# Two-layer graph network: heads, output and norm of the attention layer for two tiles at once, in stages

## The chip, the cores and the metric

The kernel runs on one core of one Trainium2 chip. The metric is the device time in microseconds (us), the median over runs. Below, DVE is VectorE, ACT is ScalarE, POOL is GpSimd, PE is TensorE, and SP is SyncE, whose queue issues plain loads.

## The reference, cut to what matters

There are 4096 nodes of 128 features and a symmetric 0/1 adjacency of 4096 x 4096 with some 64 neighbours in a row. Layer 0 is graph attention with 8 heads, layer 1 takes quantiles over each node's kept neighbours.

```python
Wh = jnp.einsum('nd,hde->hne', nodes, W)
f1 = jnp.einsum('hnd,hd->hn', Wh, a1); f2 = jnp.einsum('hnd,hd->hn', Wh, a2)
e = jax.nn.leaky_relu(f1[:, :, None] + f2[:, None, :], negative_slope=ALPHA)
att = jax.nn.softmax(jnp.where(mask, e, -9e15), axis=-1)
h = jax.nn.elu(jnp.einsum('hnm,hmd->hnd', att, Wh))
cat = jnp.transpose(h, (1, 0, 2)).reshape(N, NHEADS * DIM)
x = jax.nn.elu(cat @ W1 + b1)
out = _layernorm(nodes + x, gamma, beta)      # layer 0; layer 1 follows
```

Layer 1 gathers each node's neighbours in `out`, sorts them feature by feature, takes three quantiles, and applies one matrix and a residual.

## The kernel before, in words

Layer 0 is `gat`, layer 1 is `sparse`; a flag that is read between them chooses `sparse` (or a dense path that isn't run here), so no instruction of `sparse` starts before `gat` has ended. The change touches `gat` and the class `Front` alone.

*The front* (`Front`) turns adjacency into neighbour lists. `scan(t)` (L352) loads a tile of 128 rows in four quarters on SP's queue, makes 0/1 of them on ACT (a Relu at L361 that looks for negative entries, and a sign at L368), and packs 16 columns into one word with 16 products on PE into one PSUM buffer (L370). `first` (L379) draws the largest words of a tile on DVE in 13 rounds of a maximum and a replacement (`drain8`, L175). `second` peels the bits of four (or three) tiles, a last drain makes lists, and `place(b)` (L427) ranks the nodes of a block of 4 or 6 tiles by their neighbour count and scatters their lists by rank into `rows_d` (L519, POOL). `pieces` (L682) makes a list of these steps; `advance(2)` issues two of them after each half tile of the attention, `through(0)` all of block 0 ahead of it.

*The attention* goes over 32 tiles of 128 ranked nodes, each in two halves, u = 0 to 63. A half has four groups of 16 nodes; a group has 8 partitions a node and r neighbour rows in each (r = 7 to 13, by the block's bounds). `load(u)` (L845) gathers one row for each partition with an indirect DMA on POOL's queue (L858), 28 to 45 of them a half, 2250 in all, into buffers that hold two groups (`nb`, five buffers of up to 24 rows). The indices come from `rows_d` through SP's queue (`indices`, L816: `ids` at L823, `info` at L828). `own_row` (L835) gathers a tile's own rows. `probabilities` (L905) is the softmax: logits on DVE (L935), leaky ReLU with ACT (L943), maxima, an exponential on ACT (L955), sums over a node's 8 partitions. `rows_sum` (L963) spreads the probabilities into matrices of up to 7 rows a time on DVE (L974, two buffers) and multiplies them with the gathered rows on PE (L981) into `ps_z`, which ACT copies to `zT` (L994). After the second half `combine` (L1000) applies the heads' matrices (L1007), ELU (`elu`: a minimum on DVE, an exponential on ACT at L1245, a sum and maximum on DVE), the output matrix (L1010), the second ELU, the norm, and scatters the tile's result into `x1_d` (L1037, POOL).

*What sets the order.* Each engine takes its instructions in one order that is fixed at compile time from the program's order and from when inputs and buffers are expected to be free; independent steps of the front fill in. POOL's and SP's queues are in order as well. `issue_after` holds a half's softmax on DVE and ACT behind the sums of the half before, or behind the whole of `combine`. `load(u + 3)` is issued ahead of half u. An `nb` buffer is free again when PE has multiplied its rows.

The main loop:

```python
for u in range(2 * NT):
    t, half = divmod(u, 2)
    if u + 3 < 2 * NT:
        held[u + 3] = load(u + 3)
        if half and t + 2 < NT:
            mes[t + 2] = own_row(t + 2)
    with ExitStack() as order:
        for ins in behind:
            order.enter_context(tc.issue_after(ins))
        if not half:
            f1 = spread_f1(t, mes[t])
            zT = tp.tile([P, H, P], F32, name="zT", bufs=1)
        e = probabilities(u, held[u], f1)
    behind = rows_sum(u, held.pop(u), e, zT)
    if half:
        behind = combine(t, mes.pop(t), zT)
    advance(2)
```

Of the kernel before, what the change touches and what calls it, by code (L numbers as in the profile page):

```python
# [38 lines left out]
F32 = mybir.dt.float32  # L39
F16 = mybir.dt.float16  # L40
BF = mybir.dt.bfloat16
# [54 lines left out]
SPREAD = 7  # L96
# [206 lines left out]
class Front:  # L303
# [3 lines left out]
    def __init__(self, tc, nc, c, adj, meta_d, ctx):  # L307
# [3 lines left out]
        self.psum_w, self.psum_c = pool("fr_ps", 2, space=PSUM), pool("fr_ps1", 1, space=PSUM)  # L311
# [40 lines left out]
    def scan(self, t):  # L352

        nc = self.nc
        ps_w = self.psum_w.tile([P, NG1], F32, name="ps_words")
        quarter = N // 4
        for i in range(4):
            a_i = self.tp.tile([P, quarter], I32, name="a_i", bufs=3)
            nc.sync.dma_start(out=a_i, in_=self.adj[ts(t, P), ts(i, quarter)])
            nz = self.tp.tile([P, quarter], BF, name="nz", bufs=3)  # L360
            nc.scalar.activation(  # L361
                nz,
                a_i,
                AF.Relu,
                scale=-1.0,
                accum_out=self.negative[:, 4 * t + i : 4 * t + i + 1],
            )
            nc.scalar.sign(nz, a_i)  # L368
            for b in range(4):
                nc.tensor.matmul(  # L370
                    ps_w,
                    self.pows[:, 4 * i + b, :],
                    nz[:, ts(b, NG1)],
                    start=i + b == 0,
                    stop=i + b == 6,
                )
        self.words[t] = ps_w
# [49 lines left out]
    def place(self, b):  # L427
# [47 lines left out]
        for lhs, to in ((self.every, sums[0]), (self.before, inside)):  # L475
            ps = self.psum_c.tile([P, max(BLOCKS) * NC], F32, name="ps_c")
# [191 lines left out]
    def verdict(self, flag_d):  # L668
# [5 lines left out]
        ps = self.psum_c.tile([P, max(BLOCKS) * NC], F32, name="ps_c")  # L674
# [7 lines left out]
    def pieces(self, order_d, flag_d):  # L682

        out = []
        scans = iter(range(NT))
        ahead = lambda: [self.scan(t) for t in [next(scans, None)] if t is not None]
        out.append((None, ahead))
        for b, n in enumerate(BLOCKS):
# [7 lines left out]
            while at < START[b] + n:  # L696
# [9 lines left out]
                for j in range(m):  # L706

                    def one_(t=at + j, j=j, bufs=bufs, start=start):
                        if j == 0:
                            start()  # L710
                        ahead()
# [33 lines left out]
def gat(tc, nc, c, x, adj, xf_d, meta_d, order_d, flag_d, w, a1, a2, w1, b1, gamma, beta, x1_d):  # L745

    block = [b for b, n in enumerate(BLOCKS) for _ in range(n)]
# [15 lines left out]
    pair = max(r[i] + r[i + 1] for r, _, _ in halves_ for i in (0, 2))  # L765
    top = [max(halves_[2 * t][0] + halves_[2 * t + 1][0]) for t in range(NT)]
    with ExitStack() as ctx:
# [18 lines left out]
        rowp = ctx.enter_context(tc.tile_pool(name="ga3", bufs=5))  # L786
# [4 lines left out]
        nc.scalar.dma_start(out=w1_sb, in_=w1.rearrange("(h e) o -> e h o", e=D))  # L791
        bc = {}
        for name, src in (("b1", b1), ("gamma", gamma), ("beta", beta)):
# [8 lines left out]
        small = psum.tile([P, NJ + 2 * GR * H + D], F32, name="ps_small")  # L802
        own = small[:, :NJ]
        ps_y = small[:, NJ + 2 * GR * H :]
# [11 lines left out]
        def indices(b):  # L816
# [17 lines left out]

        def own_row(t):  # L835
            me = tp.tile([P, XF], F32, name="me", bufs=3)
            nc.gpsimd.indirect_dma_start(
                out=me,
# [4 lines left out]
            return me  # L843

        def load(u):  # L845
            t, half = divmod(u, 2)
            if half == 0 and t in START:
                indices(START.index(t))
            ids, first, r_most, _ = index[t]
            pairs = []  # L850
            gathers[u] = []
            for g, r in enumerate(halves_[u][0]):
                if g % 2 == 0:
                    pairs.append(rowp.tile([P, pair, D + H], F32, name="nb"))
                    at = 0
                for i in range(r):
                    k = first + (half * HALF + g) * r_most + i
                    gather = nc.gpsimd.indirect_dma_start(  # L858
                        out=pairs[-1][:, at, :],
# [5 lines left out]
                    at += 1  # L865
            return pairs

        def spread_f1(t, me):
# [6 lines left out]
                me[:, D + H :].unsqueeze(1).to_broadcast(shape),  # L875
# [29 lines left out]
        def probabilities(u, pairs, f1):  # L905
# [24 lines left out]
            at = 0  # L930
            for i, rows in enumerate(pairs):
                k = 0
                a, z = r[2 * i : 2 * i + 2]
# [1092 lines left out]
```

## Time and profile before

| what | us |
|---|---|
| median of nine runs (7981.03 to 7984.82) | 7983.44 |
| the profiled execution | 7989.73 |
| its span, first to last instruction | 7987.9 |
| DVE busy, of the span | 5950.9 (74%) |
| POOL busy | 4422.0 (55%) |
| ACT busy | 2197.3 (28%) |
| PE busy, products | 1024.7 (13%) |
| POOL's first neighbour gather starts | 175.34 |
| the last result scatter of `gat` starts | 3220.76 |
| first info gather of `sparse` (L1598) | 3225.14 |

Busy time counts an instruction's own duration; what an engine waited for is told in the columns of idle time, with the instruction or DMA that ended the wait. "issue" there is idle time in which the engine waited for nothing that the profile shows. A gather's row on POOL is the writing of its DMA descriptors; its data land 2.5 us (median) after the issue.

### The profile page before, as it was taken

Reading aid. Unit: us, or ns where it says so; the run is one execution under the profiler, and the core shown is the slowest. Engines: PE = TensorE matmul, PEld = TensorE weight load, DVE = VectorE, ACT = ScalarE, POOL = GpSimd, SP = SyncE. Lnnn points to the kernel's source line nnn. Section 1 sums busy time; section 2 is a strip of 40 time slices with the busy share of each in tenths; the row PEclk is TensorE's granted clock in tenths of the full one; section 3 lists DMA queues with packets and bytes.
Section 4 is the critical chain, followed back from the end, with each engine's and each line's share of the span. In section 5 each row is a group of like instructions: output and inputs, shape, how many; then the busy total and the mean of one; then the engine's idle time right before and its main releaser. Section 6 shows DMA issues by size and latency. Waiting matters only on the chain. (4 is left out here: it accounts for less than half of the span.)

```text
span 7987.9 us, 31927 instructions
## 1 busy us (share of the span) xinstructions
PE 1024.7 (13%) x6307; PEld 900.2 (11%) x6307; DVE 5950.9 (74%) x9880; ACT 2197.3 (28%) x2168; POOL 4422.0 (55%) x4564
## 2 busy tenths in 40 slices
PE   3232332322332322000000000000000000000000
PEld 2232332322222322000000000000000000000000
DVE  7575665832333332399889999999988999999999
ACT  5121221000000000133333333333333333333333
POOL 1777767777777777645535353535445444554500
PEclk5676666666666666555555555555555555555555
DMA  5333342222222222111101010101111011110100
GB/s 177 86 101 89 89 113 62 57 48 56 57 56 56 56 56 54 45 30 37 36 24 40 25 40 26 41 23 39 29 30 36 25 28 30 37 34 26 34 1 1
DMA packets 222584, 385.27 MB, mean 48 GB/s; under 512 B 121509, under 2 KB 133416, under 8 KB 222376
## 3 DMA queue, kind: packets, MB, share of 16 engines
q0 software_dynamic: 145664, 305.55, 14.8%
q1 hardware_dynamic: 64258, 70.19, 2.9%
q10 hardware_dynamic: 12454, 7.41, 0.3%
q14 instruction: 157, 1.29, 0.1%
q8 instruction: 51, 0.84, 0.0%
HBM read 372.54 MB, written 10.31 MB: 48 GB/s over the span
## 5 line engine op out<-in xcount | busy, mean ns | idle before, releaser
L1490 POOL DMA_INDIRECT rows<-x_d,info x2078 | 2046.4, 985 | 2048.9 <-DVE agg L1573 1034.0
L858 POOL DMA_INDIRECT nb<-xf_d,ids x2250 | 2145.4, 954 | 712.9 <-issue 649.8
L1524 ACT COPY low<-rows 128x2048 f32<-128x2048 f32 (+9 forms) x1009 | 1548.1, 1551 | 2548.7 <-DVE rows L1526 2209.9
L1525 DVE TENSOR_TENSOR rows<-low,rows 128x2048 f32<-128x2048 f32 (+9 forms) x1009 | 1878.0, 1886 | 210.0 <-ACT low L1524 206.9
L1526 DVE TENSOR_TENSOR rows<-low,rows 128x2048 f32<-128x2048 f32 (+9 forms) x1009 | 1876.1, 1884 | 2.7
L981 PE MATMUL ps_z<-spread,nb 128*128 128x128 f32 x4500 | 706.3, 324 | 1585.1 <-DVE spread L974 1584.9
L981 PEld LDWEIGHTS ps_z<-spread,nb 128*128 128x128 f32 x4500 | 660.1, 234 | 1635.8 <-issue 1422.5
L935 DVE TENSOR_TENSOR e<-nb,ps_small 128x144 f32<-128x144 f32 (+9 forms) x148 | 40.5, 279 | 943.8 <-DMA nb<-xf_d,ids 885.7
L1580 PE MATMUL low<-idf,com 128*128 128x128 f32 x32 | 15.2, 473 | 4700.7 <-DVE rows L1526 3836.3
L974 DVE TENSOR_TENSOR spread<-e,ps_small 128x896 f32<-128x896 f32 (+4 forms) x486 | 352.9, 765 | 247.9 <-PE ps_z L981 246.3
L1580 PEld LDWEIGHTS low<-idf,com 128*128 128x128 f32 x32 | 5.8, 182 | 4710.0 <-DVE rows L1526 3535.3
L1587 POOL DMA_INDIRECT out<-o,info x32 | 40.2, 1256 | 503.2 <-DVE o L1586 497.4
L994 ACT COPY zT<-ps_z 128x512 f32<-128x512 f32 x64 | 37.3, 584 | 950.5 <-PE ps_z L981 950.5
L943 ACT ACTIVATE ps_e<-e 128x256 f32<-128x256 f32 (+4 forms) x64 | 26.2, 409 | 981.3 <-DVE e L935 948.9
L1524 ACT COPY low_s<-rows 128x256 f32<-128x256 f32 (+3 forms) x321 | 144.8, 470 | 397.6 <-DVE rows L1525 238.0
L361 ACT ACTIVATE nz<-a_i 128x1024 bf16<-128x1024 int32 x128 | 134.1, 1048 | 364.6 <-DMA a_i<-in_adj 213.1
L179 DVE MAX8 k<-key 128x8 f32<-128x256 f32 x416 | 168.7, 414 | 1.8
L1525 DVE TENSOR_TENSOR rows<-low_s,rows 128x256 f32<-128x256 f32 (+3 forms) x321 | 156.9, 499 | 1.4 <-ACT low_s L1524 0.7
L1526 DVE TENSOR_TENSOR rows<-low_s,rows 128x256 f32<-128x256 f32 (+3 forms) x321 | 156.9, 499 | 0.4
L181 DVE MATCH_REPLACE8 key<-k,key 128x256 f32<-128x256 f32 x384 | 156.3, 408 | 0.0
L370 PE MATMUL ps_words<-nz,pows 128*128 128x256 bf16 x512 | 104.7, 361 | 293.4 <-ACT nz L368 143.8
L1528 DVE TENSOR_TENSOR rows<-rows 128x256 f32<-128x256 f32 (+8 forms) x245 | 139.0, 581 | 0.1
(219 smaller groups left out, 2495.6 us busy)
## 6 DMA issues: line engine op xcount, KB each, us to landing
a_i<-in_adj SPq DMA_DIRECT2D x128, 512.0 KB, 4.6
nb<-xf_d,ids POOLq DMA_INDIRECT x2250, 2.5
rows<-x_d,info POOLq DMA_INDIRECT x2078, 2.5
xf_d<-xf ACTq DMA_DIRECT2D x4, 576.0 KB, 7.3
xf<-in_x ACTq DMA_DIRECT2D x4, 512.0 KB, 8.5
meta_d<-rowdata_k SPq DMA_DIRECT2D x4, 324.0 KB
abc_ta<-in_L_gnn_a ACTq DMA_DIRECT2D x2, 512.0 KB, 9.2
w_ga<-in_L_gnn_W ACTq DMA_DIRECT2D x2, 512.0 KB
```

The lines of the kernel that those rows point to most:

```text
L179: nc.vector.max(out=top, in_=work)
L181: nc.vector.match_replace(out=work, in_to_replace=top, in_values=work, imm_value=gone)
L361: nc.scalar.activation(nz, a_i, AF.Relu, scale=-1.0, accum_out=self.negative[:, 4 * t + i : 4 * t + i + 1],)
L370: nc.tensor.matmul(ps_w, self.pows[:, 4 * i + b, :], nz[:, ts(b, NG1)], start=i + b == 0, stop=i + b == 6,)
L858: gather = nc.gpsimd.indirect_dma_start(out=pairs[-1][:, at, :], out_offset=None, in_=xf_d, in_offset=bass.IndirectOffsetOnAxis(ap=ids[:, ...
L974: last = nc.vector.tensor_tensor(spread[:, :m], e[:, at : at + m, :].unsqueeze(2).to_broadcast(shape), own.unsqueeze(1).unsqueeze(3).to_br ...
L981: product = nc.tensor.matmul(ps_z[:, g, :], pairs[g // 2][:, k + i, :D], spread[:, i].rearrange("p j h -> p (j h)"), start=i0 + i == 0, st ...
L1490: nc.gpsimd.indirect_dma_start(out=row, out_offset=None, in_=x1_d, in_offset=bass.IndirectOffsetOnAxis(ap=info[:, col : col + 1], axis=0),)
L1524: nc.scalar.copy(packed, lows)
L1525: nc.vector.tensor_tensor(lows, packed, highs, op=ALU.min)
L1526: nc.vector.tensor_tensor(highs, packed, highs, op=ALU.max)
L1528: nc.vector.tensor_tensor(lows, lows, highs, op=ALU.min)
```

## The change

It does this:

- `scan` takes two tiles from tile 2 on: one PSUM buffer holds the words of both, and each of the 16 products covers both (512 columns instead of 256).
- `rowp` has six buffers of 18 rows. Two neighbouring groups share one where they fit into 18 rows, else each has its own.
- Spreads take up to 9 rows, in equal parts, with three buffers. The sums have two PSUM buffers.
- The softmax of half u + 1 is issued right after the sums of half u; the copy of the sums to `zT` comes behind it (`collect`), then one stage of each pair of tiles under way, then two steps of the front.
- `combine` works on two tiles at once (256 columns) and in stages: heads in two lots, output, transposes, norm, result scatter. One stage is taken per half, so a pair's scatters come up to six halves after its last sums. The output is now computed transposed, with the bias added by ACT, and turned back by two transposes.
- Own rows are gathered ahead of their tile's first half, into buffers for two tiles, of which there are five.
- The small PSUM areas of the front and the attention share one bank.

The core of the diff:

```diff
-SPREAD = 7
+ROWS = 18
+SPREAD = 9
+TWO = 2
...
-    def scan(self, t):
+    def scan(self, t, m):
-        ps_w = self.psum_w.tile([P, NG1], F32, name="ps_words")
+        ps_w = self.psum_w.tile([P, 2, NG1], F32, name="ps_words")
...
+            nz = self.tp.tile([P, 2, quarter], BF, name="nz", bufs=2)
+            for j in range(m):
...
                 nc.tensor.matmul(
-                    ps_w,
+                    ps_w[:, :m, :],
                     self.pows[:, 4 * i + b, :],
-                    nz[:, ts(b, NG1)],
+                    nz[:, :m, ts(b, NG1)],
...
-        scans = iter(range(NT))
+        scans = [(0, 1), (1, 1)] + [(t, 2) for t in range(2, NT, 2)]
+        def ahead(t):
+            while scans and scans[0][0] <= t + 1:
+                self.scan(*scans.pop(0))
...
-        rowp = ctx.enter_context(tc.tile_pool(name="ga3", bufs=5))
+        rowp = ctx.enter_context(tc.tile_pool(name="ga3", bufs=6))
...
+                me = tp.tile([P, TWO, XF], F32, name="me", bufs=5)
...
+            for g in range(HALF):
+                if where and g % 2 and r[g - 1] + r[g] <= ROWS:
+                    where.append((where[-1][0], r[g - 1]))
+                else:
+                    where.append((rowp.tile([P, ROWS, D + H], F32, name="nb"), 0))
...
+            ps_z = psum.tile([P, HALF, NJ * H], F32, name="ps_z", bufs=2)
+                parts = -(-r // SPREAD)
+                for i0 in range(0, r, -(-r // parts)):
+                    m = min(-(-r // parts), r - i0)
+                    spread = tp.tile([P, SPREAD, NJ, H], F32, name="spread", bufs=3)
...
+        def combine(t, zT):
+            n = TWO * P
+            def product(h0):
+                ps_h = bank().rearrange("p (k n) -> p k n", n=n)
+                for k in range(TWO):
+                    nc.tensor.matmul(
+                        ps_h[:, k, :], w_sb[:, h0 + k, :], zT[:, h0 + k, :], start=True, stop=True
+                    )
+                return ps_h
+            pending = []
+            for h0 in range(0, H, TWO):
+                if len(pending) == 2:
+                    yield
+                    for h, ps_h in pending:
+                        elu(nc, zT[:, h : h + TWO, :], ps_h)
+                    pending = []
+                pending.append((h0, product(h0)))
+            yield
+            for h, ps_h in pending:
+                elu(nc, zT[:, h : h + TWO, :], ps_h)
+            ps_y = bank()[:, :n]
             for h in range(H):
+                nc.tensor.matmul(ps_y, w1_sb[:, h, :], zT[:, h, :], start=h == 0, stop=h == H - 1)
+            yield
+            yT = tp.tile([P, n], F32, name="yT", bufs=1)
+            nc.scalar.activation(yT, ps_y, AF.Identity, bias=b1_sb)
+            y = bank()[:, :n].rearrange("p (t o) -> p t o", o=D)
+            for j in range(TWO):
+                nc.tensor.transpose(y[:, j, :], yT[:, ts(j, P)], c["idf"])
+            yield
...
+            yield
+            for j in range(TWO):
+                nc.gpsimd.indirect_dma_start(
+                    out=x1_d,
...
+        held = {u: load(u) for u in range(3)}
         advance(EARLY)
+        f1s = {0: spread_f1(0)}
+        e, _ = probabilities(0, held[0], f1s[0])
+        going = []
         for u in range(2 * NT):
...
+            if not half and t + 1 < NT:
+                f1s[t + 1] = spread_f1(t + 1)
+            ps_z, behind = rows_sum(u, held.pop(u), e)
+            if u + 1 < 2 * NT:
+                with ExitStack() as order:
+                    for ins in behind:
+                        order.enter_context(tc.issue_after(ins))
+                    e, behind = probabilities(u + 1, held[u + 1], f1s[(u + 1) // 2])
             with ExitStack() as order:
                 for ins in behind:
                     order.enter_context(tc.issue_after(ins))
+                if u % (2 * TWO) == 0:
+                    zT = tp.tile([P, H, TWO * P], F32, name="zT")
+                collect(u, ps_z, zT)
+                for stages in going:
+                    next(stages, None)
+            if u % (2 * TWO) == 2 * TWO - 1:
+                going = going[-1:] + [combine(t - 1, zT)]
             advance(2)
+        for stages in going:
+            for _ in stages:
+                pass
```

## The prediction

> **What bounds the kernel now.** I read the time slices of the page first. Each digit is the busy tenth of a slice of 199.7 us; the last three fifths are the second layer (`sparse`), where DVE is full.
>
> ```profile
> DVE  7575665832333332399889999999988999999999
> POOL 1777767777777777645535353535445444554500
> ```
>
> The change touches only the first layer (`gat`), so everything from the first info gather of `sparse` (L1598, 3225.1 us) to the end is taken as it is: 7987.9 - 3225.1 = 4762.8 us. What counts is when `gat` ends. In slices 2 to 16 neither row is at 9. So I asked for busy times from the first neighbour gather to the end of the last (columns: busy us and count of PE, PEld, DVE, ACT, POOL, then clock, DMA share, GB/s), and for POOL's groups in the same stretch.
>
> ```profile
> 175.00:3186.00 3011.00, 907.38 (x5835) 820.90 (x5833) 1424.59 (x5499) 406.43 (x650) 2264.66 (x2373) 0.66 0.28 71
> ```
> ```profile
> L858 POOL DMA_INDIRECT nb<-xf_d,ids x2250 | 2145.4, 954 | 712.9 <-issue 649.8 <-PE ps_z L981 25.3 <-DMA nb<-xf_d,ids 23.5
> ```
>
> POOL is busy for 75%, DVE for 47%. But of POOL's 713 us idle ahead of gathers, 650 are "issue": 0.30 us ahead of each of the 2,250. POOL's own order of time shows gathers every 1.25 us, and only two breaks over 0.5 us in this stretch: 4.9 us before the first gather (for its indices), and this one:
>
> ```profile
> 1029.09 0.96 POOL L519 DMA_INDIRECT rows_d<-rowdata,pos_i  x1 [0.30 <-issue]
> 1030.36 0.96 POOL L1037 DMA_INDIRECT x_d<-s,info  x1 [0.31 <-issue]
> 1054.18 0.98 POOL L858 DMA_INDIRECT nb<-xf_d,ids  x1 [22.86 <-PE ps_z L981]
> ```
>
> So from 175 to 3184 us POOL's queue is full: 2,373 indirect DMAs at 1.25 to 1.26 us each, 2,983 us, plus that one stall. DVE's largest wait says the same from the other side: it waits for gathers.
>
> ```profile
> DVE e L935 <- DMA nb<-xf_d,ids: 879.4, 62, 49.3
> ```
>
> Here the Trainium skill speaks for the change, and the row against it. "Perfetto Trace Analysis", Optimization Strategy, says that the same gap repeating on an engine that should be saturated can mean too few buffers. The 0.30 us gap repeats, but it is there from 175 to 212 us too, where every `nb` buffer is still empty. By the rule a sixth buffer could win part of 650 us; by the row, nothing.
>
> **The change, part by part.** The chain is: time to the first gather, POOL's queue, the tail from the last gather to the last row written.
>
> (1) *The gathers* stay 2,250, with 32 own rows, 32 rank scatters, 32 order scatters and 32 result scatters. Heads, output and norm for two tiles, sums copied later, spreads of 8 or 9 rows in one instruction (before: 7 + 1 at 1082 + 279 ns, 7 + 2 at 1082 + 412 ns) save DVE some 0.12 us for each of about 180 groups, 22 us, and the norm in pairs about 2 us per tile, 70 us. All of it lies beside POOL's queue while DVE waits 879 us for gathers: worth 0. If that cover were gone it would be worth those 90 us.
>
> Two moved steps add a wait. The copy of a half's sums (L994) now stands on ACT behind the exponential of the next half, so up to 45 us, a half's gathers, later; behind it on ACT are the scans' Relus and the heads' input. Nobody on POOL's path waits for it, since the sums get a second PSUM buffer and free the `nb` buffers through PE, not through the copy: 0; without the second buffer it would be 45 us a half. The row factors of the next tile (L873) are issued ahead of the sums of this one and wait for that tile's own row. In POOL's order of time own rows are 100 to 120 us ahead of the end of their half's gathers, and the change has buffers for ten tiles of them instead of three: 0; if they came just in time, DVE would hold back the sums by up to 45 us in every second half.
>
> (2) *Words for two tiles per product* (start). DVE begins the key of tile 1 at 67.5, tile 2 at 77.0, tile 3 at 86.2 us (L382), and one drain of 13 rounds alone takes 0.98 us a round (34 to 36 us), two interleaved 0.72 a round (77 to 82 us). With tiles 2 and 3 in one product both come at about 87: tile 1 alone ends at 67.5 + 13 x 0.98 = 80, then some 7 us of nothing, then 26 x 0.72 = 19 us, to 106. Before, the second peel (L210) began at 101.4, with one round of tile 3 left. The rank scatter at 165.5 and the first gather at 175.3 move with it: **+4 us**; bounds -4 (the drain of tile 4, which filled holes, leaves them free) and +12 (all of the 7 idle us, and the fill still in the way).
>
> (3) *POOL's stalls* are the uncertain term. The 22.9 us arose so: the rank scatters of the next block (L519) stand in POOL's queue behind all gathers that had a free buffer; SP's index load (L823) waits for them; behind it wait adjacency loads; ACT stands at a Relu without its input; behind it waits the exponential of the half under way, and its sums must free the buffer that POOL wants. The waits of ACT and SP show it (columns: us in total, times, longest):
>
> ```profile
> ACT nz L361 <- DMA a_i<-in_adj: 202.8, 14, 70.7
> ```
> ```profile
> SPq L823 <- DMA rows_d<-rowdata,pos_i: 229.7, 4, 78.3
> ...
> SPq L828 <- DMA x_d<-s,info: 95.4, 2, 81.1
> ```
>
> In ACT's order of time it stood 59, 71 and 66 us for adjacency words (at 380, 756 and 1039 us) and 67 us at 1385, where DVE waited 59.5 us for the rank scatters (L510). Once in four this outlasted POOL's buffers. The change gives six buffers of 18 rows for five of 24, 20 us more cover for halves of 7 to 9 rows a group. But groups of 10 or more no longer share one (10 + 10 > 18): in the last two halves of each block a half takes four buffers, which leaves two loaded ahead, 20 or 21 gathers, 25 us. In the quiet stretch the first spread comes 8.3 us after the last gather and the first buffer is free about 15 us after it: no stall. In the front stretch (to 1600 us) spreads follow 12 to 15 us after it, more where front pieces lie between, and now two front pieces, the ELU of the pair and the heads' products are issued between a half's softmax and its sums, where before they came after the sums. A first drain or a second peel is 10 to 20 us: buffer free at 30 to 45 us against 25 us of cover, a stall of 5 to 20 us. And the result scatter now comes up to six halves later; the info tile of block 2 has two buffers, so SP's L828 waits for the scatter of tile 3, which is now at half 13, just where block 2 is loaded: a new head of SP's queue (that wait was 81 us at most before). A stall of the kind seen costs 23 us wherever it hits, since it runs from the landing of the scatters through ACT, softmax and sums. Bounds: 0 (the sixth buffer covers all) and 130 us (each of four block changes a 23 us stall, three wide pairs 13 us each). I take 45 us, two such stalls, nearer to today's 28 (22.9 + 4.9) than to the upper end, since three changes of four had no stall: **+17 us**.
>
> (4) *The tail.* Now:
>
> ```profile
> 3184.49 0.98 POOL L1037 DMA_INDIRECT x_d<-s,info  x1 [0.30 <-issue]
> ...
> 3220.76 0.97 POOL L1037 DMA_INDIRECT x_d<-s,info  x1 [35.28 <-DVE s L1036]
> ```
>
> Between them: softmax to 3193.9; sums 3195.15 to 3209.2, 14.0 us for 90 records that stream at 0.125 us; copy 0.6; heads and ELU 4.2; output 2.1; norm 5.1. After: three spread buffers let PE stream, 90 x 0.125 = 11.3 us, **-2.7** (0 to -3). Four banks of two heads over 256 columns through two PSUM buffers: a bank's ELU chain is 0.69 + 0.63 + 0.68 and 0.1 of hand-over, two rounds of it with a product of 0.5 to 1.0 us between, output on 256 columns: **+2.5**. The output is now transposed: ACT 0.45, two transposes 0.5 and hand-over, less the addition of 0.29: **+0.9**. ELU, five norm steps and the scaling on 256 columns (0.41 to 0.45 us for 0.29): **+1.6**. A second scatter behind the first: **+1.3**. The stages of tiles 28 and 29 that are still open, some 4.4 us of DVE, lie mostly beside PE's 11 us: **+2** (0 to 4.4). Two scatters less stand ahead of the last gather, 2 x 1.25: **-2.5**. Sum **+3 us** (-2 to +9).
>
> Where (2) to (4) add up: +4 + 17 + 3 = +24 us. The profiled execution took 7989.7 us, 1.8 more than its span and 6.3 more than the median of the nine runs; 8014 by its own measure, **8007 us by the median 7983.4**.
>
> **The rivals.** *A, my forecast (0.46):* the stalls grow; start and tail cost 7. Its own range is +17 to +95, 8000 to 8078. For it: the second wait ahead of SP, the wide halves. Against it: the sixth buffer.
>
> *B, no change that shows (0.36):* POOL's queue stays as full as now, stalls of 10 to 35 us, so +7 - 18 to +7 + 7, centre about 7987 us. This is also what comes if the new order is not kept: the compiler's list order already moves pieces about (own rows are issued 100 to 120 us ahead of the half that needs them), and the queues could end up as before. For it: 2,373 issues that nothing removes.
>
> *C, faster (0.18):* one mechanism: the sixth buffer carries POOL through every block change, and 27.8 us of stalls go but for the 4.9 at the start. With the start at 0 instead of +4: -22.9 + 3 = -20, 7963 us. It decides from where the buffer free times stay under 82 us after a narrow half's last gather (two halves of gathers) and 25 us after a wide one's. For it: at 1054 us another 20 us of buffer would have covered nearly all of the 23. Against it: only 16 us or more of this 20 would show.
>
> **How the numbers follow.** 0.2% of this kernel, 16 us, is about what a measurement can tell from no change; slower by more is A (0.46), within it B (0.36), faster by more C (0.18). The likeliest is A at its centre, 8007. Bounds added up: down -4 - 28 - 2 = -34 with all at their best, up +12 + 102 + 9 = +123 with all at their worst; for 8 in 10 I cut to 7963 (C's centre) and 8070, leaving about a tenth on each side.
>
> **What would show it.** The first gather at 177 to 183 us; gathers still 1.25 us apart; breaks in POOL's queue that name sums' matmuls, at tiles 3, 7, 13 and at the block changes up to 1600 us, 45 us in all; none after 1700 us; the last scatter some 38 to 44 us after the last gather; `sparse` unchanged at 4763 us. I am wrong if POOL's step differs from 1.25 us, if the number of gathers does, or if the breaks vanish (C) or exceed 130 us: then the order of the front pieces against the sums is what I misjudged.

## The result, and the profile after

The changed kernel takes 8009.77 us (median of ten runs, 8008.13 to 8011.72); the kernel before took 7983.67 us beside it (30 runs). The ratio is 1.0033, 95% interval 1.0025 to 1.0041: slower by 26 us, a third of a per cent. The profiled execution has a span of 8011.5 us, 23.6 more than the 7987.9 of before.

Where do 23.6 us come from? The page first, DVE and POOL in slices of 200.3 us:

```profile
DVE  6555556555222222399889999899988999999999
POOL 1777777777777777645435353635445444554500
```

The picture is the same: POOL at 7 up to 3.2 ms, then DVE at 9. The second layer took 4763.9 us from its first info gather (L1657) to the end, before 4762.8. So the loss lies ahead of it. Next the busy times of the stretch of gathers (columns as in the prediction), and POOL's gathers in it:

```profile
175.00:3186.00 3011.00, 875.48 (x5154) 759.89 (x5154) 1337.04 (x5064) 345.39 (x578) 2256.27 (x2366) 0.62 0.28 69
```
```profile
L886 POOL DMA_INDIRECT nb<-xf_d,ids x2246 | 2139.9, 953 | 695.4 <-issue 652.2 <-DMA nb<-xf_d,ids 20.1 <-PE ps_z L1008 8.1
```

PE, DVE and ACT have less to do in this stretch (DVE 88 us less); POOL has the same things to issue, but for two result scatters that now come later, at the same 0.95 + 0.30 us. DVE's idle time as a whole grew by the 88 us that it saved. Two of its waits grew by more, and others shrank: it waits 1233.3 us for gathers (885.7 in the same stretch of the kernel before), and 192.9 us, in eight places, for own rows ahead of the row factors. The kernel before, then the changed one:

```profile
DVE mine L873 <- DMA me<-xf_d,info: 26.1, 2, 22.7
```
```profile
DVE e L962 <- DMA nb<-xf_d,ids: 1233.3, 99, 32.4
DVE mine L900 <- DMA me<-xf_d,info: 192.9, 8, 48.8
```

What did change is POOL's breaks. Before there was one of 22.9 us; now there are twelve over 0.5 us, 34.0 us in all. Here are three of them within 25 us, in POOL's order of time (start, duration, what ended the idle time ahead of it):

```profile
888.43 0.99 POOL L1094 DMA_INDIRECT x_d<-s,info  x1 [0.30 <-issue]
890.97 0.97 POOL L1094 DMA_INDIRECT x_d<-s,info  x1 [1.54 <-DMA x_d<-s,info]
896.04 1.00 POOL L862 DMA_INDIRECT me<-xf_d,info  x1 [4.10 <-DMA info<-rows_d]
...
910.36 0.97 POOL L886 DMA_INDIRECT nb<-xf_d,ids  x1 [7.05 <-PE ps_z L1008]
```

These are the three kinds of break. A pair's second result scatter waits for the first to land (seven times, 1.5 to 2.0 us; an eighth, of 3.2 us at the same place, names a DVE instruction). Own rows wait 4.1 us for their indices (three times: 896, 1336 and 1899 us), and SP's own order of time shows why: the info load (L847) goes out at 893.28, just after that scatter has landed. And one gather waits 7.05 us for a buffer, the only break of over 0.5 us that names the sums' matmul. DVE's order of time shows what these sums (half 14) had waited for:

```profile
898.67 0.23 DVE L900 TENSOR_TENSOR mine<-me,group 128x64 f32<-128x64 f32 x1 [20.12 <-DMA me<-xf_d,info]
...
903.94 0.81 DVE L1001 TENSOR_TENSOR spread<-e,ps_small 128x640 f32<-128x640 f32 x1
```

DVE stood for 20.1 us at the row factors of the next tile, which need the own row that came late, and the spreads come behind them. Counted out from the trace, PE is done with the first buffer of this half 48 us after the half's last gather; in the other five halves up to 1600 us whose groups all have 10 rows or more it is 23 to 31 us.

The other part is the tail. The last gather ends at 3191.18 us; then (all engines, in order of time):

```profile
3204.25 6.11 PE L1057 MATMUL ps_h<-zT,w_ga 128*128 128x256 f32 x16
3210.20 9.76 PE L1008 MATMUL ps_z<-spread,nb 128*128 128x128 f32 x86
...
3220.00 0.59 ACT L1023 COPY zT<-ps_z 128x512 f32<-128x512 f32 x1 [9.13 <-PE ps_z L1008]
...
3231.91 0.99 POOL L1094 DMA_INDIRECT x_d<-s,info  x1 [40.73 <-DVE s L1091]
...
3243.26 0.95 POOL L1094 DMA_INDIRECT x_d<-s,info  x1 [2.21 <-DMA lw<-in_L_gnn_W]
```

The output product of tiles 28 and 29 (L1057) stands on PE ahead of 86 of the last 90 sums, and four scatters, those of 28 and 29 (3231.91 and 3234.44) and those of 30 and 31 (3240.10 and 3243.26), end the layer. From the last gather's end to the last scatter's start it is 52.1 us, before 36.6.

The account, in us of the two profiled executions:

| | before | after | difference |
|---|---|---|---|
| first gather starts | 175.34 | 178.56 | +3.2 |
| breaks over 0.5 us up to the last gather | 22.9 (1) | 34.0 (12) | +11.2 |
| eleven normal gaps that these breaks replace, 0.30 each | | | -3.4 |
| issues from first to last gather | 2372 | 2370 | -2.5 |
| mean duration of an issue, x 2370 | 0.9543 | 0.9537 | -1.4 |
| last gather ends (sum) | 3184.19 | 3191.18 | +7.0 |
| from there to the first info gather of `sparse` | 40.96 | 56.43 | +15.5 |
| from there to the end | 4762.8 | 4763.9 | +1.1 |

### The profile page after: what moved, and what is told of

Same layout as the page of the kernel before. It is cut to its first block, busy times and chain, and to the rows that moved or that the text cites. A ratio compares the mean times of both kernels' runs of the same rounds, so it can differ in the third digit from the quotient of the medians.

```text
span 8011.5 us, 29926 instructions
## 1 busy us (share of the span) xinstructions
PE 1001.4 (12%) x5587; PEld 837.0 (10%) x5587; DVE 5868.3 (73%) x9452; ACT 2152.8 (27%) x2120; POOL 4417.1 (55%) x4564
## 3 DMA queue, kind: packets, MB, share of 16 engines
q14 instruction: 153, 1.25, 0.1%
## 5 line engine op out<-in xcount | busy, mean ns | idle before, releaser
L962 DVE TENSOR_TENSOR e<-nb,ps_small 128x144 f32<-128x144 f32 (+8 forms) x166 | 43.4, 264 | 1323.7 <-DMA nb<-xf_d,ids 1249.8
L1008 PE MATMUL ps_z<-spread,nb 128*128 128x128 f32 x4500 | 612.5, 304 | 769.2 <-DVE spread L1001 760.5
L1008 PEld LDWEIGHTS ps_z<-spread,nb 128*128 128x128 f32 x4500 | 600.9, 219 | 803.1 <-DVE spread L1001 380.1
L1001 DVE TENSOR_TENSOR spread<-e,ps_small 128x1152 f32<-128x1152 f32 (+4 forms) x312 | 342.6, 1106 | 86.6 <-PE ps_z L1008 84.3
L1646 POOL DMA_INDIRECT out<-o,info x32 | 39.8, 1244 | 506.0 <-DVE o L1645 500.2
L900 DVE TENSOR_TENSOR mine<-me,group 128x64 f32<-128x64 f32 x32 | 6.8, 212 | 196.1 <-DMA me<-xf_d,info 192.9
L376 PE MATMUL ps_words<-nz,pows 128*128 128x512 bf16 (+1 forms) x272 | 111.7, 567 | 286.3 <-ACT nz L374 191.7
```

What stands on the lines that cost most here:

```text
L376: nc.tensor.matmul(ps_w[:, :m, :], self.pows[:, 4 * i + b, :], nz[:, :m, ts(b, NG1)], start=i + b == 0, stop=i + b == 6,)
L1001: last = nc.vector.tensor_tensor(spread[:, :m], e[:, at : at + m, :].unsqueeze(2).to_broadcast(shape), own.unsqueeze(1).unsqueeze(3).to_br ...
L1008: product = nc.tensor.matmul(ps_z[:, g, :], rows[:, k + i0 + i, :D], spread[:, i].rearrange("p j h -> p (j h)"), start=i0 + i == 0, stop=i ...
```

## The experiments

Theory 1 is the account read as causes: POOL's queue is the chain, its new breaks come from two waits that the change added (scatter behind scatter; scatter, info load, own row), and the tail is longer by the serial work of a pair and by the open stages of tiles 28 and 29. The rival, theory 2, is the prediction's: buffers come free too late (breaks that name the sums' matmul), whatever the scatters do.

The first four experiments ran together; before took 7984.4 us beside them (30 runs), 0.7 us more than beside the changed kernel, so their differences to the changed kernel are good to about 1 us. Each undoes one thing.

### Words one tile at a time

```diff
-        scans = [(0, 1), (1, 1)] + [(t, 2) for t in range(2, NT, 2)]
+        scans = [(t, 1) for t in range(NT)]
```

> The changed kernel with adjacency words scanned one tile at a time again (products of 256 columns). Theory P (prediction, term 2): tiles 2 and 3 in one product come out later and push the first gather; undone, the first gather comes at about 175.3 us instead of 178.56, and the whole kernel ends about 3 us earlier, near 8006; the breaks in POOL's queue stay. Rival Q: products of half the width cost PE and ACT twice the instructions in the front stretch, the adjacency words of later tiles come later and POOL breaks longer: the 3 us come back as breaks, or more (8010 to 8030). Rival R: the start was moved by something else in the change: first gather still at 178 to 179.

Measured: 8006.84 us, ratio to before 1.0027 (1.0017 to 1.0038). The first gather, at 174.50, is 4.1 us earlier than in the changed kernel and the time 2.9 us shorter; the breaks are 35.6 us instead of 34.0. So the two-tile words cost their 3 us at the start and save nothing later that shows.

### Three info buffers

```diff
-            info = tp.tile([P, max(BLOCKS), 2], I32, name="info")
+            info = tp.tile([P, max(BLOCKS), 2], I32, name="info", bufs=3)
```

> The changed kernel with three buffers for the info tile instead of two (nothing else). After has three breaks of 4.1 us ahead of own rows (L862 waiting for the info load, which waits for a result scatter). Theory P: the load can go before the scatter of the tile that used the buffer, so these three breaks go, 12.3 us, and SP's wait for the scatters (450 us in all, longest 339) shrinks; the time falls by 8 to 12 us to about 7999, less what the next break takes up. Rival Q: SP's queue still stands at the next thing, the rank scatters, and the own row waits about as long: breaks stay at 34 us in all, time unchanged within 3 us. Rival R: the loads that come sooner let POOL run into its buffers at the block changes: breaks named by the sums' matmul come back at about 20 us, time unchanged or up to 15 us longer.

Measured: 7989.51 us, ratio 1.0006 (0.9997 to 1.0015). One buffer of 12 numbers per partition is worth 20 of the 26 us. The waits of SP in the stretch of gathers, first in the kernel before, then in the changed kernel, then in this one (total, times, longest), and POOL's order of time at the place shown above:

```profile
SPq L828 <- DMA x_d<-s,info: 188.1, 3, 92.7
```
```profile
SPq L847 <- DMA x_d<-s,info: 827.5, 6, 370.9
```
```profile
SPq L847 <- DMA x_d<-s,info: 27.9, 1, 27.9
```
```profile
897.28 0.99 POOL L1094 DMA_INDIRECT x_d<-s,info  x1 [0.31 <-DVE pw L204]
899.82 0.97 POOL L1094 DMA_INDIRECT x_d<-s,info  x1 [1.55 <-DMA x_d<-s,info]
901.10 0.98 POOL L886 DMA_INDIRECT nb<-xf_d,ids  x1 [0.30 <-issue]
```

No own row holds POOL back any more, and the break of 7.05 us that named the sums is gone, together with DVE's wait of 20.1 us ahead of it. In the three other experiments here both stay (DVE waits 18.4 to 20.6 us, POOL breaks 6.2 to 8.0). Breaks in all: 10.0 us instead of 34.0, and none over 1.3 us ahead of a neighbour gather. That is more than the 12.3 us of the own rows, and more than theory 1 asked for: the buffer break stood behind the late load, by way of the row factors, and three second scatters no longer stand right behind a first one. DVE still waits 170.4 us for own rows at other places; no break of POOL over 1.3 us ahead of a gather comes of it. The stretch of gathers (2990.0 us) is now 18.8 us shorter than in the kernel before (3008.9), 2.5 of it for two scatters that now come behind it. Of theory 2 there remains this: its breaks were 7.05 us, and they came of the late load.

### Independent result scatters

The rows that the scatters write are a permutation, so none needs the one before it.

```diff
-                nc.gpsimd.indirect_dma_start(
+                done = nc.gpsimd.indirect_dma_start(
...
+                for other in results:
+                    tc.declare_no_dep(done.ins, other, reason="the places are a permutation")
+                results.append(done.ins)
```

> The changed kernel with the result scatters declared independent of each other, so that a second scatter doesn't wait for the landing of the first. Theory P: the eight breaks of 1.5 to 3.2 us ahead of a second scatter go (11 us less 8 normal gaps of 0.3: some 12 us of 34), and in the tail, where four scatters stand in a chain, 2 to 6 us; time about 10 to 16 us less, 7994 to 8000. Rival Q: the break only moves to the next instruction of POOL, because what comes behind waits for the same landing or a buffer: breaks in all stay at 30 to 34 us, and only the tail's 2 to 6 us are won. Rival R: the tail is not set by the scatters but by the norm's chain on DVE ahead of them: tail (last gather to last scatter) 50 us or more as in after (52.1).

Measured: 7999.18 us, ratio 1.0018 (1.0009 to 1.0027), 10.6 us less than the changed kernel. In the tail a pair's scatters now go out back to back. The first pair:

```profile
3221.43 0.99 POOL L1094 DMA_INDIRECT x_d<-s,info  x1 [40.44 <-DVE s L1091]
3222.73 0.97 POOL L1094 DMA_INDIRECT x_d<-s,info  x1 [0.30 <-issue]
```

The last pair's do too (1.26 us from start to start for 3.16): the 2.21 us ahead of the last scatter, which the profile of the changed kernel puts down to a load of weights, were the wait for the landing.

All eight breaks of second scatters are gone, 14.7 us with their normal gaps, but 6.5 us came back at other places (buffer and own-row breaks 25.8 us in all): 8.2 us won in the stretch (theory P said some 12), 3.2 us from the last gather to the first info gather; the time is where P put it. Rival R's 50 us are missed by a tenth: the last scatter is still 49.9 us behind the last gather, so most of the tail is not the scatters.

The Trainium skill has the price behind these breaks: "DMA: Bandwidth & Descriptors", Anatomy of one DMA, puts some 2 us of fixed cost on a DMA, most of it until the write's receipt is back. The trace agrees: from one scatter's start to a waiting one's it is 2.54 us (888.43 to 890.97), without the wait 1.30.

### Tiles 28 and 29 finished early

```diff
                 for stages in going:
-                    next(stages, None)
+                    for _ in range(3 if u >= 2 * NT - 4 else 1):
+                        next(stages, None)
```

> The changed kernel, taking three stages of the pairs under way per half in the last four halves, so that tiles 28 and 29 are finished before the last sums. Theory P: the open stages of 28 and 29 (their output product on PE ahead of the last sums, their norm on DVE between the last pair's) cost some 10 us of the tail's 52.1; done early they lie beside gathers: tail 40 to 44 us, sums copied 25 us after the last gather instead of 28.8, time about 7999 to 8002. Rival Q: the serial chain of the last pair itself (four banks of ELU, output, transposes, norm on 256 columns) is the tail; then the tail stays at 48 us or more and the time within 4 us of after. Rival R: the stages pulled forward put ELU and output between softmax and sums of halves 60 to 63, the nb buffers come free later, and POOL breaks there for 5 to 15 us: tail shorter, time unchanged.

Measured: 8003.77 us, ratio 1.0024 (1.0015 to 1.0033), 6.0 us less than the changed kernel. The stretch of gathers is as in the changed kernel (breaks 34.0), the tail 45.4 us. The order of time after the last gather (its end at 3186.66):

```profile
3197.68 12.13 PE L1008 MATMUL ps_z<-spread,nb 128*128 128x128 f32 x90 [49.95 <-DVE spread L1001]
...
3209.85 0.58 ACT L1023 COPY zT<-ps_z 128x512 f32<-128x512 f32 x1 [14.98 <-PE ps_z L1008]
...
3228.75 0.96 POOL L1094 DMA_INDIRECT x_d<-s,info  x1 [37.77 <-DVE s L1091]
```

With 28 and 29 out of the way the sums are one row of 12.1 us (before 14.0) and are copied 23.2 us behind the last gather, 1.8 us sooner than in the kernel before. The rest is the pair's own chain: 18.9 us from that copy to the first scatter (before 11.6), and 3.3 from there to the second. Tail and time come out 1.4 and 1.8 us above theory P's ranges, and outside rival Q's. So both halves of theory 1's tail hold: 6.7 us were the open stages, the other 8.8 the pair's chain (7.3 + 3.3 - 1.8).

### A second kind of chip

The remaining eight runs were made on four other chips, and none of these is like the one of the first four runs. On each of them the kernel before itself takes 9054 to 9107 us, with all its runs on one chip within 0.5%. "Kind" is a name for this: that it lies in the chip was not shown. POOL breaks so often there that its full queue is no longer what bounds the kernel. What these runs say of the change on the first kind is little; what they say of the second kind is worth having. First the expectations, which were made for the first kind.

All four edits together:

> The changed kernel with all four edits at once: words one tile at a time, three info buffers, independent result scatters, tiles 28 and 29 finished before the last sums. Theory P (the losses stand one behind the other on POOL's queue and its tail, so they add): alone they gave -3, -20, -11 and -6 us against 8009.8; together 7968 to 7976, breaks in the stretch of gathers under 8 us instead of 34, first gather at 175, tail 43 to 46 us. Rival Q (they cover each other: what one break gives up, the next takes): 7980 to 7990, breaks of 15 us or more left. In both the tail stays longer than the 36.6 us of before.

The kernel before with a sixth buffer of 24 rows (`rowp` with bufs=6), and the same again on another chip:

> The kernel before with six nb buffers of 24 rows instead of five, nothing else. Theory P (rival C of the prediction: one more buffer carries POOL through the block change): the break of 22.9 us at 1054 goes, or falls below 6 us; time 7983 - 17 to 7983 - 23, 7960 to 7967. Rival Q (the stall runs from the rank scatters' landing, wherever it hits, and an extra buffer only moves it): a break of 15 to 23 us at another place, time 7978 to 7986.

> The same kernel as b_bufs6 (before with six nb buffers of 24 rows), again, since before itself took 9091 us on the chip of that call, where POOL broke 115 times, so that the run could not tell the theories apart. Theory P (one more buffer carries POOL through the block change): the break of 22.9 us at 1054 goes or falls below 6 us, 7960 to 7967 where before takes 7983. Rival Q (an extra buffer only moves the stall): a break of 15 to 23 us at another place, 7978 to 7986.

The changed kernel with five buffers (bufs=5):

> The changed kernel with five nb buffers of 18 rows instead of six. Theory P (the sixth buffer is what keeps the stalls named by the sums' matmul at 7 us): a wide half takes four of five buffers, so breaks named by the sums come back at the wide halves of blocks 1 to 3 and the block changes, 10 to 25 us each, 40 to 130 us in all, time 8045 to 8130. Rival Q (the new order of the work, not the buffer, removed the stall): breaks named by the sums stay under 20 us, time 8010 to 8025.

The kernel before with each gather of own rows made twice:

```diff
+            spare = tp.tile([P, XF], F32, name="spare", bufs=3)
+            for to in (spare, me):
-            nc.gpsimd.indirect_dma_start(
-                out=me,
+                nc.gpsimd.indirect_dma_start(
+                    out=to,
...
```

> The kernel before with the gather of each tile's own rows issued twice, the second into a buffer that nothing else uses: 32 more indirect DMAs on POOL, no more work elsewhere. Theory P (POOL's queue is full at 1.26 us an issue, though it is 75% busy): 32 x 1.26 = 40 us more, 8020 to 8027; first gather to last gather 3049 us instead of 3009. Rival Q (the 0.30 us gaps are slack that a longer queue would use up): under 10 us more, 7984 to 7994. Rival R (DMA bandwidth or the wait for landed rows is the bound): 32 x 128 rows more in 2,373 x 128, under 1.4% of the stretch, 40 us at most, but with the gap between issues grown, not their number.

The four edits with tiles 30 and 31 combined singly, 512 // 128 heads in a bank, and the last four tiles' stages taken ahead of the next softmax:

> The changed kernel with words one tile at a time, three info buffers and independent result scatters, and with the last four tiles taken out of the new order: tiles 28 and 29 are finished before the softmax of the half after them, tiles 30 and 31 each get heads, output and norm by themselves (four heads over 128 columns in a bank), tile 30 ahead of the last softmax. Theory P (the three waits and the tail are all that the change costs, and they stand one behind the other): first gather at 175, breaks in the stretch of gathers under 8 us, tail (last gather to last result scatter) 35 to 39 us as in before instead of 52.1; time 7960 to 7968 on a chip where before takes 7983. Rival Q (the tail of a pair is longer by its own chain, transposes and all, whatever else is open): tail 42 to 46 us, 7968 to 7975. Rival R (breaks return elsewhere): breaks of 15 us or more, 7976 or above.

| run | us | before there | ratio (95%) | breaks, us | tail, us |
|---|---|---|---|---|---|
| all four edits | 8654.6 | 9091.2 | 0.9515 (0.9501 to 0.9528) | 695 | 43.0 |
| changed, five buffers | 8633.2 | 9091.2 | 0.9498 (0.9484 to 0.9512) | 654 | 52.1 |
| before, six buffers | 9099.3 | 9091.2 | 1.0014 (1.0005 to 1.0024) | 1116 | 81.2 |
| before, own rows twice | 9106.8 | 9091.2 | 1.0014 (1.0004 to 1.0023) | 1107 | 64.5 |
| last four tiles singly | 8642.6 | 9054.0 | 0.9554 (0.9536 to 0.9572) | 661 | 41.9 |
| before, six buffers, again | 9065.8 | 9054.0 | 1.0019 (1.0008 to 1.0031) | 1090 | 79.6 |

Here the changed kernel with one buffer fewer is 5% faster than before. With six buffers and all four edits it is no faster than that (8654.6 for 8633.2 on the same chip); with six and no edit it was not run there. A sixth buffer wins nothing for the kernel before, and 32 more gathers cost 16 us (4 to 21), not 40. Every time and every sum of breaks that was expected failed, for one reason: POOL breaks 74 to 120 times instead of once or twelve times. (The first gather and the tail of 43.0 us with all four edits came as expected.) All that the runs of this kind can say is what is late there. The kernel before with six buffers, all engines, in order of time:

```profile
2516.78 3.27 PE L981 MATMUL ps_z<-spread,nb 128*128 128x128 f32 x16
...
2539.09 0.94 POOL L858 DMA_INDIRECT nb<-xf_d,ids  x1 [0.30 <-issue]
2545.93 1.42 DVE L974 TENSOR_TENSOR spread<-e,ps_small 128x896 f32<-128x896 f32 x2 [27.60 <-remote]
2546.22 0.95 POOL L858 DMA_INDIRECT nb<-xf_d,ids  x1 [6.19 <-remote]
```

PE is done with the spread buffer at 2520. DVE, with nothing else to do, starts the next spread at 2545.93: 5.9 us after POOL has issued its last gather (2540.0), and POOL itself gets its buffer 0.3 us later ("remote" means that the profile has no record of the release). Of DVE's 45 idle times of over 10 us between 1700 and 4200 us ahead of a spread, a first ELU step or the output's addition, 34 ended with POOL quiet for over 1 us, the other eleven while POOL was still issuing; PE had then been idle for 25 us (median). In the kernel before on the first kind of chip no such idle time between 1700 us and the last gather reaches 10 us. The work itself is no slower: a spread takes 763 ns here and 762 there, a gather 949 and 954. So theory S: on these chips PE's word that it is done reaches DVE and POOL (and ACT, for which no row here shows it) late for as long as POOL issues at full rate.

Two runs put it to the test. The kernel before with six buffers and a third spread buffer:

> The kernel before with six nb buffers of 24 rows and three spread buffers instead of two. On a chip where before takes 7983: theory P (rival C of the prediction: one more buffer carries POOL through the block change): the break of 22.9 us at 1054 goes or falls below 6 us, and the last sums get 0 to 3 us shorter; 7957 to 7967. Rival Q (an extra buffer only moves the stall): a break of 15 to 23 us at another place, 7976 to 7986. On a chip where before takes 9050 to 9090, with breaks of 1090 us in POOL's queue: theory S (there PE's word to DVE and ACT that it is done with a buffer comes late for as long as POOL issues, and each such round costs): a third spread buffer saves one round of some eight in each half, breaks 30 to 150 us less than with two (1090 to 1116), time 8930 to 9050. Rival T (it is the exponentials or the gathered rows that come late there, not PE's word): breaks of 1080 us and more as with two, 9050 to 9110.

Measured: 8995.75 us beside 9099.16, ratio 0.9887 (0.9871 to 0.9904), breaks 1006 us. One spread buffer, worth at most 3 us by the prediction's account of the first kind of chip, is worth 103 here, together with a sixth buffer that alone is worth nothing. That is as S said, and against T: what frees the spread buffers is among what is late. It doesn't show that POOL's issuing is the cause; the breaks are compared with those of two other chips. And the kernel with the last four tiles singly, with four spread buffers of 8 rows:

> As a_best (words one tile at a time, three info buffers, independent result scatters, the last four tiles out of the new order), with four spread buffers of 8 rows instead of three of 9. On a chip where before takes 7983: theory P (the three waits and the tail are all that the change costs, and they add): first gather at 175, breaks in the stretch of gathers under 8 us instead of 34, tail 35 to 40 us instead of 52; 7958 to 7968, faster than both kernels; the spreads of 9 rows in two instructions cost nothing, since DVE waits for gathers. Rival Q (breaks return elsewhere): 15 us of breaks or more, 7976 or above. On a chip where before takes 9050 to 9100: theory S (PE's word to DVE and ACT comes late while POOL issues, and each buffer round that waits for it costs): a fourth buffer leaves fewer rounds that wait, breaks under 620 us instead of 661, ratio to before 0.935 to 0.953 instead of 0.955. Rival T (not the rounds of the spread buffers): 661 us of breaks or more, since groups of 9 rows now take two spreads; ratio 0.955 to 0.97.

Measured: 8675.01 beside 9106.81, ratio 0.9526 (0.9513 to 0.9539), breaks 710 us. The ratio is where S put it, the breaks are where T put them, on another chip than the run it is compared with: it tells nothing apart.

Where the changed kernel's 5% come from on these chips is suggested by what DVE waits for in the stretch of gathers. The kernel before with six buffers, then the changed kernel with five:

```profile
DVE spread L974 <- remote: 658.6, 57, 34.6
DVE y L1012 <- remote: 428.3, 20, 35.1
DVE cat L1244 <- remote: 411.5, 35, 33.0
```
```profile
DVE spread L1001 <- remote: 631.0, 44, 40.6
```

The waits ahead of the heads' ELU and the output's addition, 840 us, are not among the waits of the changed kernel with five buffers: there a stage's products are a half old when DVE takes them up. By theory S a late word costs nothing where nobody stands waiting for it. That the stages, and not the pairs, do this was not tried by itself.

## Why the prediction was right, and where not

The time was forecast at 8007 and came out at 8009.8, the sum at +24 and +23.6. The direction and the chain were understood. That the sum fits so closely is luck: two of its terms were off by about 10 us in opposite directions.

- **The bound.** POOL's queue is the chain, at 0.95 + 0.30 us per issue: the account above closes to 0.1 us with POOL's terms alone. The gap is 0.3048 us with five buffers, 0.3048 with six and 0.3047 with three info buffers, so the repeated gap, which by the rule weighed in the prediction could mean too few buffers, doesn't.
- **(1) Work beside POOL's queue.** Less work on DVE, worth 0, was right by the account: DVE is 82.6 us less busy over the whole span (forecast some 90) and waits more. That it would stay 0 if the work were doubled was not tried. The other 0 was wrong: own rows were taken to come 100 to 120 us early, so that the row factors of the next tile never wait for them. DVE waited for them 192.9 us in eight places. Only one of these, the 20.1 us at 898.67, is followed by a break of POOL that names the sums, the 7.05 us.
- **(2) The start, +4:** +3.2, and undone it gives back 2.9 in time. The mechanism was right: the words of tiles 2 and 3 come at 86.36 us (forecast 87), after 6.49 us of nothing (some 7).

```profile
86.36 0.76 DVE L389 SCALAR_TENSOR_TENSOR key<-ps_words,iota_g 128x256 f32<-128x256 f32 x2 [6.49 <-PE ps_words L376]
```

- **(3) POOL's stalls, +17:** +7.8 (11.2 less the normal gaps), and mostly by another path. I expected 45 us of breaks that name the sums' matmul, at wide halves and block changes; there were 7.05 us of these, and 1.2 with the third info buffer. The step that failed is that buffers of wide halves in the front stretch come free 30 to 45 us after the half's last gather, against 25 us that two loaded buffers cover. The first of them came free 23 to 31 us after it (at 31 us a pair of scatters and its wait stood in between, so POOL lost nothing more), and 48 us after it only in the half that DVE's wait for an own row held back.

  The break of 22.9 us went, as rival C said; whether the sixth buffer took it or the new order of the work is open, since the changed kernel with five buffers was not run on the first kind of chip. C's time failed because of waits that it left out.

  The info tile was named in the prediction, as a new head of SP's queue. The path from there was wrong: not through adjacency words, ACT and the sums to a buffer, but straight to POOL, whose next instruction was an own row that needs that load, and once through DVE's row factors. And the waiting of the second scatter for the first's landing was priced only in the tail, 1.3 us once, though every pair pays it where nothing stands between its scatters (seven of fourteen in the stretch of gathers).

  Nor is the 17 like for like: it is 45 less 27.8, and 4.9 of the 27.8 stand ahead of the first gather and stayed (4.4). Counted as in the account, 45 us of breaks are +22, and the forecast sum +29.
- **(4) The tail, +3 with the two scatters fewer:** +13.0 counted so (15.5 less 2.5). The sums gained 1.9 us (12.1 for 14.0; forecast 2.7) where they were free to. What was mis-sized: the open stages of 28 and 29, +2 in the prediction, cost 6.7, since their output product stands on PE ahead of the sums, and not only beside them on DVE, and their norm then alternates on DVE with the last pair's. The pair's chain from copy to first scatter, +5.0 in the prediction, costs +7.3; by the rows of the run with tiles 28 and 29 finished early it is the heads (+3.5) and the output product (+1.6, 3.7 us for 2.1) that were taken too cheaply at 2.5 for both, while turning the output back (+0.7 for 0.9) and the norm (+1.6) came as forecast. The second scatter, +1.3, costs 3.3, since it waits for the landing.
- **The signs.** First gather at 178.56 (177 to 183), gathers 1.25 us apart and a second layer of 4763.9 us came as said. Not as said: the breaks that name the sums, four breaks after 1700 us (9.4 us, at scatters and an own row) where none was forecast, and a last scatter 52.1 us behind the last gather for 38 to 44.
- **Rival B** (no change that shows) is just excluded by the interval; the changed kernel with a third info buffer lies where B put the time.

What is left open: whether all four edits together beat the kernel before on the first kind of chip. By their own effects (2.9 + 20.3 + 10.6 + 6.0 = 39.8 us) it would be near 7970 if they add; no run there shows it. Nor was a sixth buffer in the kernel before, or five in the changed one, seen there.

## What to carry to other kernels

When work is taken later, look for every small tile whose buffer is held until then: here twelve numbers per partition, kept for a scatter six halves later, held back a load, and through it the queue that bounds the kernel, and one more buffer gave back three quarters of the loss. Ask the same of small inputs that the new order wants earlier: an own row that came late made an engine with time to spare hold back the sums. An instruction that is issued in pairs on the bounding queue must not wait for its twin, so say that they are independent when they are. And price the tail by what is in front of each engine's last piece, not by the last piece alone.

## What the runs showed of the hardware

- The same program takes 7984 us on the chip of the first four experiments and 9054 to 9107 on four others. Its gathers and spreads last as long there (949 and 763 ns for 954 and 762, with a sixth buffer), the second layer nearly so (4777 us for 4763). The changed kernel, a third of a per cent slower in the first place, is 5% faster in the second, with five buffers or with the edits above. What is late there are starts that wait for PE: in the rows shown DVE starts 26 us after PE's last product. Why is not known here.
- POOL takes 0.95 us, and 0.30 until the next, for every indirect DMA of 128 rows, on both kinds of chip; in the changed kernel 2,370 of them fill 2,983 us of the first layer. The Trainium skill's page "DMA: Bandwidth & Descriptors", Anatomy of one DMA, calls the making of descriptors small; for these the measurement decides.
- Of POOL's breaks that go when the thing they name is mended, others can go with them (24.0 us for 12.3 named) or come in their place (8.2 for 14.7).
